# The first 128 columns of the keys' weights as a transfer of their own on ScalarE's queue, in a cross-attention and mixture-of-experts kernel

## The chip, the cores and the metric

The kernel runs on one core of a Trainium2 chip. The metric is the device time of one execution in microseconds (us). A core has five engines that run side by side: TensorE (PE in the profile, its weight loads as PEld), VectorE (DVE), ScalarE (ACT), GpSimd (POOL) and SyncE (SP), which here only issues DMAs. SP, ScalarE and GpSimd can each issue DMAs into a queue of their own; the data is moved by sixteen DMA engines that all queues share. Engines wait for one another, and for DMAs, on semaphores.

## What is computed

Four sequences of 1024 tokens of 256 values attend to a context of 77 rows with 16 heads of 64 values, and the result goes through a mixture of nine experts, of which each token takes two. The part that matters here is the setup of the attention: the context is layer-normed and multiplied with the keys' weights (the first 1024 columns of `Wkv`).

```python
xn = layernorm(x, ln1_w, ln1_b)          # x is the context here, 4 x 77 x 256
ln = layernorm(latents, ln2_w, ln2_b)    # the tokens
q = ln @ Wq
kv = xn @ Wkv
k, v = jnp.split(kv, 2, axis=-1)
...
q = q * (1.0 + scale[:, None, :, None]) + shift[:, None, :, None]
qk = jnp.einsum('bihd,bjhd->bhij', q, k) * attn_scale
attn = jax.nn.softmax(qk, axis=-1)
out = jnp.einsum('bhij,bjhd->bihd', attn, v)
...
x = x + out.reshape(b, -1, INNER) @ Wout
x = x + ffn(layernorm(x), Wr, Wg, Wu, Wd)   # nine experts, the best two of each token
```

All of it is in 32-bit floats.

## The kernel before

The order of the work is written out by hand: each engine executes its instructions in the order in which the program issues them, and only semaphores hold it. There are three stages. The setup, up to about 60 us, folds all weights of the attention into two tables for each sequence, `g` (from context to scores) and `u` (from scores to the output), so that the second stage needs only a few products for each of its 32 blocks of 128 tokens. The third stage runs the experts over lists of tokens that the second stage has written, with the experts' weights streaming in.

The change lies in the first ten microseconds of the setup. What happens there, in order:

- SP issues the loads: the context `cx` in two halves (L381, 77 partitions x 2 x 256 each), the keys' weights `wk_sb` (L382, 128 partitions x 2 x 1024, so 1 MB), the queries' weights `wq_sb` (L383), the values' weights `wv_sb` (L384) and the output's weights `wo_sb` (L385), 1 MB each. L is the line in the kernel.
- ScalarE issues the two small rows `crows` (the context's layer norm, L362) and `frows` (scale and shift, L363), then loads an activation table with a first activation `junk` (L366). Later it issues `wrow` (L473).
- GpSimd issues `qb`, `wr_sb`, `wr_last` and a fill of the token lists in DRAM.
- TensorE runs products on zeros to warm its clock (`warm`, L159), five at once and three more behind `pc` (L418), the turned `crows`.
- VectorE takes the context's statistics (`cst` L404, `cmv` L406), ScalarE the root (`csd` L410), VectorE the reciprocal and most of the normed context `cn` (L456 to L463), ScalarE one quarter of it (L468). TensorE turns it (`pct`, L479), and `cT`, its first half by ScalarE (L488) and its second by VectorE (L483), is what the products need.
- For each of eight pairs of heads, n = 0 to 7, TensorE makes `pk` (L515) of 128 columns of `wk_sb`, from n * 128 on, and `cT`. ScalarE copies the product to `kT` (L519), VectorE scales it into `kTs` (L520). From the fifth pair on, the queries' weights are turned between the pairs (`pwq`, L431), the first reader of `wq_sb`.
- Then come the products for `g` (`pgk`, L651), for `brow` and `u`, up to the first scores at 63 us.

A tile is one block of memory with a name; the tiles `crows`, `frows`, `wrow`, `wq_sb`, `wk_sb` and `cx` come from one pool, `kside`. A read waits for the write of just the part of the tile that it reads. The DMAs of SP and ScalarE share eight semaphores in turn; a DMA that takes a semaphore again waits at its issue until the earlier DMA on it has landed. So `wo_sb` waits at SP for the first half of the context.

The reading side of the weights is this loop:

```python
for n in range(NP):
    pk = bank_tile(f"pk{n}")
    for c in range(C):
        nc.tensor.matmul(
            pk[:, : B * J], wk_sb[:, c, n * P : (n + 1) * P], cT[:, c, :],
            start=(c == 0), stop=(c == C - 1),
        )
```

Of the kernel before, what the change touches and what calls it, by code (L numbers as in the profile page):

```python
# [8 lines left out]
F32 = mybir.dt.float32  # L9
# [6 lines left out]
P = 128  # L16
# [5 lines left out]
def kernel(  # L22
# [18 lines left out]
    nc = tc.nc  # L41
# [4 lines left out]
    INNER = wq.shape[1]  # L46
    DH = INNER // H
    E, _, FF = wg.shape
    C = D // P
# [306 lines left out]
    with tc.tile_pool(name="vside", bufs=1) as vside, ExitStack() as kvs:  # L356
        kside = kvs.enter_context(tc.tile_pool(name="kside", bufs=1))

        crows = kside.tile([2, D], F32, name="crows")
        frows = kside.tile([2, B, NP], F32, name="frows")  # L360
        for k, src in enumerate((ln1_w, ln1_b)):
# [5 lines left out]

        wrow = kside.tile([P, D], F32, name="wrow")
        wq_sb = kside.tile([P, C, INNER], F32, name="wq_sb")
        wk_sb = kside.tile([P, C, INNER], F32, name="wk_sb")  # L370

        QT = 4
        brow = vside.tile([P, NP // QT, B * J], F32, name="brow")
# [5 lines left out]
        for i in range(2):  # L379
            at = slice(i * BH, (i + 1) * BH)  # L380
            nc.sync.dma_start(out=cx[:J, at], in_=ctx_in[at].rearrange("b j d -> j b d"))  # L381
        nc.sync.dma_start(out=wk_sb, in_=wkv[:, :INNER].rearrange("(c p) n -> p c n", p=P))  # L382
        nc.sync.dma_start(out=wq_sb, in_=wq_v)  # L383
        nc.sync.dma_start(out=wv_sb, in_=wkv[:, INNER:].rearrange("(c p) n -> p c n", p=P))  # L384
        nc.sync.dma_start(out=wo_sb[:, :, :D], in_=wout.rearrange("(n p) d -> p n d", p=P))  # L385
# [75 lines left out]
        for b in range(B):  # L461
# [12 lines left out]
            out=wrow, in_=ln2_w.rearrange("(o d) -> o d", o=1).to_broadcast([P, D])  # L474
# [123 lines left out]
        for i in range(2):  # L598
# [4 lines left out]
            out=before, in_=ones, pattern=[[1, P]], compare_op=ALU.is_gt, fill=0.0, base=0,  # L603
# [68 lines left out]
        for b in range(B):  # L672
            nc.vector.tensor_copy(g_sb[b][:, :, HJ:], wz)
            for t in range(2):
                for k in range(NP // QT):
                    nc.sync.dma_start(
                        out=g_sb[b][P - 1 : P, C - 1, :HJ].rearrange(
                            "p (k q t j) -> p k q t j", q=QT, t=2, j=J
                        )[:, k, :, t, :],
                        in_=brow.rearrange("(q r) k m -> q r k m", q=QT)[  # L680
                            :, t * B + b, k, b * J : (b + 1) * J
                        ],
# [871 lines left out]
```

## Time and profile before

| what | us |
|---|---|
| three runs | 924.75, 927.01, 927.33 |
| their median | 927.01 |
| the profiled execution | 924.82 |
| its span, from the first to the last instruction | 922.8 |
| granted TensorE clock, mean, as a share of full speed | 0.997 |

TensorE's time by stage, from the table of stretches:

| stretch | length | TensorE busy |
|---|---|---|
| 0 to 1.5, before the first product | 1.50 | 0.03 |
| 1.5 to 8.8, warming and turning of the context | 7.30 | 7.27 |
| 8.8 to 10.6 | 1.80 | 0.01 |
| 10.6 to 32 | 21.40 | 21.40 |
| 32 to 60 | 28.00 | 28.00 |
| 60 to 480, mostly attention | 420.00 | 415.81 |
| 480 to 900, mostly experts | 420.00 | 419.60 |
| 900 to 922.8 | 22.80 | 14.56 |

In lines of groups and of the timeline, `out<-in` names the tiles, `x` the count and the bracket at the end what the engine waited for, and for how long. A time of a matmul's end is modelled. "SPq" and "ACTq" are DMA issues on SP and ScalarE: the duration is that of issuing, not of the transfer. A row of the table of stretches gives the stretch, its length, then for PE, PEld, DVE, ACT and POOL the busy time and the number of instructions, then the granted TensorE clock, the mean busy share of the DMA engines and the GB/s that they moved.

### The profile page before, as it was taken

How to read it: one execution, taken by the hardware profiler on the slowest of the kernel's cores; microseconds unless marked ns; L12 is line 12 of the kernel's file. 1: busy time of each engine (PE TensorE's matmuls, PEld its weight loads, DVE VectorE, ACT ScalarE, POOL GpSimd, SP SyncE). 2: the span in 40 equal slices, each digit the busy share in tenths (PEclk: the TensorE clock that was granted, in tenths of full speed). 3: DMA queues.
4: the chain of work that ended last, by engine and by line, in shares of the span. 5: the costliest groups of instructions: out<-in, count | busy, mean ns of one | idle time of the engine just before them, and what ended most of it. 6: DMA issues, size and time to landing. Idle time of an engine off the chain costs nothing. (4 is left out here: it accounts for less than half of the span.)

```text
span 922.8 us, 13371 instructions
## 1 busy us (share of the span) xinstructions
PE 906.7 (98%) x4210; PEld 703.5 (76%) x4210; DVE 450.0 (49%) x1330; ACT 341.7 (37%) x1075; POOL 318.2 (34%) x329
## 2 busy tenths in 40 slices
PE   8999999999999999999999999999999999999996
PEld 6676777777777777788888777777777777778885
DVE  5776678888788887763722222222222222222221
ACT  4666575565646566551211122222222222111210
POOL 5000000321504242146454445435435435444432
PEclk9999999999999999999999999999999999999998
DMA  6200010503102710456779779779779777779822
GB/s 216 70 0 1 24 46 25 46 24 46 51 30 59 229 30 24 117 153 172 179 209 299 217 207 307 212 211 313 218 205 310 219 208 227 218 220 312 226 35 23
DMA packets 109125, 137.02 MB, mean 148 GB/s; under 512 B 24247, under 2 KB 79039, under 8 KB 109056
## 3 DMA queue, kind: packets, MB, share of 16 engines
q1 hardware_dynamic: 91498, 118.78, 42.0%
q0 software_dynamic: 17344, 17.26, 10.5%
q8 instruction: 34, 0.56, 0.3%
q14 instruction: 35, 0.29, 0.1%
q10 hardware_dynamic: 214, 0.13, 0.0%
HBM read 119.48 MB, written 18.33 MB: 149 GB/s over the span
## 5 line engine op out<-in xcount | busy, mean ns | idle before, releaser
L1193 PE MATMUL pg<-xT,wgu 128*128 128x256 f32 x1144 | 251.7, 379 | 0.4 <-PEq L1510 0.4
L1193 PEld LDWEIGHTS pg<-xT,wgu 128*128 128x128 f32 x1144 | 215.9, 190 | 29.3 <-issue 0.8
L1267 PE MATMUL po<-wd,hid 128*128 128x256 f32 (+1 forms) x804 | 180.5, 379 | 0.0
L1267 PEld LDWEIGHTS po<-wd,hid 128*128 128x128 f32 (+1 forms) x804 | 147.2, 187 | 21.3 <-issue 0.7
L275 ACT ACTIVATE ex<-psc,mx 128x77 f32<-128x77 f32 x512 | 124.2, 361 | 101.8 <-DVE mx L265 96.7
L1302 POOL DMA_INDIRECT out_dram<-co,ids x63 | 100.7, 1599 | 170.4 <-DVE co L1270 136.4
L918 POOL DMA_INDIRECT list_d<-r_entry,r_pli x64 | 67.2, 1050 | 256.2 <-DVE r_pli L916 124.9
L338 PE MATMUL po<-u,aT 128*128 128x265 f32 x640 | 151.7, 391 | 0.9 <-ACT aT L327 0.8
L261 PE MATMUL psc<-g,zT 128*128 128x462 f32 (+1 forms) x384 | 139.1, 511 | 1.2 <-ACT zT L250 1.2
L338 PEld LDWEIGHTS po<-u,aT 128*128 128x128 f32 x640 | 118.7, 189 | 23.7 <-ACT aT L327 1.9
L1200 DVE TENSOR_TENSOR hid<-pg,sl 128x256 f32<-128x256 f32 x130 | 55.1, 424 | 160.0 <-ACT sl L1199 159.7
L1199 ACT ACTIVATE sl<-pg 128x256 f32<-128x256 f32 x130 | 49.8, 384 | 218.3 <-PE pg L1193 211.9
L261 PEld LDWEIGHTS psc<-g,zT 128*128 128x128 f32 x384 | 72.5, 189 | 59.2 <-issue 49.4
L1270 DVE TENSOR_SCALAR co<-po,ids 128x256 f32<-128x256 f32 x67 | 32.4, 484 | 136.2 <-PE po L1267 136.1
L1151 POOL DMA_INDIRECT yin<-y_d,ids x67 | 70.4, 1051 | 24.7 <-issue 14.7
L265 DVE TENSOR_REDUCE mx<-psc 128x6 f32<-128x462 f32 (+1 forms) x96 | 55.7, 581 | 18.1 <-PE psc L261 15.1
L295 DVE TENSOR_REDUCE sm<-ex 128x16 f32<-128x1232 f32 x32 | 45.9, 1435 | 37.1 <-ACT ex L275 37.1
L327 ACT COPY aT<-pa 128x512 f32<-128x512 f32 (+1 forms) x96 | 49.4, 552 | 26.7 <-PE pa L319 26.7
L319 PEld LDWEIGHTS pa<-ident,an 128*128 128x128 f32 x320 | 36.9, 141 | 7.7 <-PE po L338 1.4
L319 PE MATMUL pa<-ident,an 128*128 128x128 f32 x320 | 40.2, 273 | 1.0 <-DVE an L299 1.0
L299 DVE TENSOR_TENSOR an<-ex,rs 128x1024 f32<-128x1024 f32 x32 | 39.2, 1225 | 1.1
L1255 ACT COPY hid<-ph 128x384 f32<-128x384 f32 x15 | 7.2, 479 | 73.9 <-PE ph L1250 73.9
(312 smaller groups left out, 840.7 us busy)
## 6 DMA issues: line engine op xcount, KB each, us to landing
wgu<-in_L_ffn_Wg_dram SPq DMA_DIRECT2D x41, 704.0 KB
wd<-in_L_ffn_Wd_dram SPq DMA_DIRECT2D x41, 640.0 KB
wgu<-in_L_ffn_Wu_dram SPq DMA_DIRECT2D x41, 512.0 KB
wgu<-in_L_ffn_Wu_dram SPq DMA_DIRECT2D x41, 128.0 KB
x<-in_x_dram SPq DMA_DIRECT2D x8, 512.0 KB
out_dram<-x SPq DMA_DIRECT2D x8, 512.0 KB
y_d<-y SPq DMA_DIRECT2D x8, 512.0 KB
w<-in_L_ffn_Wg_dram SPq DMA_DIRECT2D x5, 704.0 KB
```

The lines of the kernel that those rows point to most:

```text
L261: nc.tensor.matmul(psc[:, :w], zT[:, c, :], g_sb[i // NS // GPB][:, c, h * J : h * J + w], start=(c == 0), stop=(c == C - 1),)
L265: nc.vector.tensor_reduce(nmx[i][:, h : h + n], psc[:, : n * J].rearrange("p (h j) -> p h j", h=n), AX.X, ALU.max, negate=True,)
L275: nc.scalar.activation(exs[i][:, h + q, :], pscs[k][:, q * J : (q + 1) * J], AF.Exp, bias=nmx[i][:, h + q : h + q + 1],)
L319: nc.tensor.transpose(pa[:, q * P : (q + 1) * P], ans[i][:, (k + q) * P : (k + q + 1) * P], ident)
L338: nc.tensor.matmul(po[:, :DE], aT[:, n, :], u_sb[b][:, n, :], start=(n == 0), stop=(n == KC - 1))
L918: i = nc.gpsimd.indirect_dma_start(out=list_d[:, :], out_offset=bass.IndirectOffsetOnAxis(ap=place_i[:, s : s + 1], axis=0), in_=entries[k ...
L1151: return nc.gpsimd.indirect_dma_start(out=dst, out_offset=None, in_=src, in_offset=bass.IndirectOffsetOnAxis(ap=offsets, axis=0), **kw,)
L1193: nc.tensor.matmul(pg[:, g, :], w[:, c, at : at + P], xT[:, c, :], start=(c == 0), stop=(c == C - 1),)
L1199: nc.scalar.activation(sl, pg[:, 0, :], AF.Silu)
L1200: nc.vector.tensor_tensor(hid[:, f, :], pg[:, 1, :], sl, ALU.mult)
L1267: nc.tensor.matmul(po[rows, :D], hid[:, f, at], d[:, f, :], start=(f == 0), stop=(f == NF))
L1302: i = nc.gpsimd.indirect_dma_start(out=out_r, out_offset=bass.IndirectOffsetOnAxis(ap=rows_of(j, h, rows), axis=0), in_=cos[j][:, h, :], i ...
```

## The change

One transfer becomes two. The first 128 columns of the keys' weights, the ones that the first pair reads, are fetched by ScalarE, as its first DMA, before `crows` and `frows`; the other 896 columns are fetched by SP where the whole was before, behind the context. For this the tile `wk_sb` is made at the head of its pool.

```diff
@@ -356,6 +356,10 @@
     with tc.tile_pool(name="vside", bufs=1) as vside, ExitStack() as kvs:
         kside = kvs.enter_context(tc.tile_pool(name="kside", bufs=1))
 
+        wk_sb = kside.tile([P, C, INNER], F32, name="wk_sb")
+        wk_v = wkv[:, :INNER].rearrange("(c p) n -> p c n", p=P)
+
+        nc.scalar.dma_start(out=wk_sb[:, :, :P], in_=wk_v[:, :, :P])
         crows = kside.tile([2, D], F32, name="crows")
         frows = kside.tile([2, B, NP], F32, name="frows")
         for k, src in enumerate((ln1_w, ln1_b)):
@@ -367,7 +371,6 @@
 
         wrow = kside.tile([P, D], F32, name="wrow")
         wq_sb = kside.tile([P, C, INNER], F32, name="wq_sb")
-        wk_sb = kside.tile([P, C, INNER], F32, name="wk_sb")
 
         QT = 4
         brow = vside.tile([P, NP // QT, B * J], F32, name="brow")
@@ -379,7 +382,7 @@
         for i in range(2):
             at = slice(i * BH, (i + 1) * BH)
             nc.sync.dma_start(out=cx[:J, at], in_=ctx_in[at].rearrange("b j d -> j b d"))
-        nc.sync.dma_start(out=wk_sb, in_=wkv[:, :INNER].rearrange("(c p) n -> p c n", p=P))
+        nc.sync.dma_start(out=wk_sb[:, :, P:], in_=wk_v[:, :, P:])
         nc.sync.dma_start(out=wq_sb, in_=wq_v)
         nc.sync.dma_start(out=wv_sb, in_=wkv[:, INNER:].rearrange("(c p) n -> p c n", p=P))
         nc.sync.dma_start(out=wo_sb[:, :, :D], in_=wout.rearrange("(n p) d -> p n d", p=P))
```

## The prediction

> **What bounds the kernel now.** I read the page first (part 1, then the slices of part 2), then the list of waits for the first 70 us, the timeline of the first 13 us, and the table of stretches for those. The page:
>
> ```profile
> span 922.8 us, 13371 instructions
> PE 906.7 (98%) x4210; PEld 703.5 (76%) x4210; DVE 450.0 (49%) x1330; ACT 341.7 (37%) x1075; POOL 318.2 (34%) x329
> ```
>
> TensorE is counted busy for all but 922.8 - 906.7 = 16.1 us. Nothing that removes waits from it can give more, and a change in the setup can only give what TensorE idles there. The waits:
>
> ```profile
> PE pk L515 <- DMA wk_sb<-in_L_xattn_Wkv_dram: 1.8, 1, 1.8
> PE warm L159 <- DVE u L155: 1.5, 1, 1.5
> ```
>
> The setup has two idle stretches on TensorE: 1.5 us of start, and 1.8 us in front of the first product with the keys' weights. Only the second concerns this change. In the table of stretches TensorE is busy for 49.00 of the 49.00 us from 11 to 60, so a shift at 11 us is passed on. How the 1.8 us come about is in the timeline (start, duration, engine, line, operation):
>
> ```profile
> 0.83 0.81 SPq L381 DMA_DIRECT2D cx<-in_ctx_dram  x2
> 0.84 0.52 ACTq L362 DMA_DIRECT2D crows<-in_L_xattn_ln_w_dram  x1
> 1.69 0.44 SPq L382 DMA_DIRECT2D wk_sb<-in_L_xattn_Wkv_dram  x1
> 3.91 1.40 DVE L404 BATCH_NORM_STATS2 cst<-cx 77x6 f32<-77x256 f32 x4 [2.23 <-DMA cx<-in_ctx_dram]
> 6.24 1.05 DVE L463 TENSOR_SCALAR cn<-cx,cmv,cr 77x256 f32<-77x256 f32 x3
> 6.33 1.56 PE L159 MATMUL warm<-u 128*128 128x256 f32 x6
> 7.73 0.70 PE L479 MATMUL pct<-ident,cn 77*128 77x77 f32 x8
> 8.20 0.61 ACT L488 ACTIVATE cT<-pct,cwb 128x308 f32<-128x308 f32 x1 [1.25 <-PE pct L479]
> 8.47 0.60 DVE L483 TENSOR_SCALAR cT<-pct,cwb 128x308 f32<-128x308 f32 x1 [1.11 <-PE pct L479]
> 10.60 2.57 PE L515 MATMUL pk<-cT,wk_sb 128*128 128x308 f32 x9 [1.83 <-DMA wk_sb<-in_L_xattn_Wkv_dram]
> ```
>
> Two inputs meet at 10.60: the turned context cT, ready at 8.20 + 0.61 = 8.81 (first half) and 8.47 + 0.60 = 9.07 (second), and wk_sb, which comes last. The trace's semaphore records put the sixteen parts of the wk_sb landing between 7.71 and 10.46. What the DMA engines did meanwhile (last columns: granted clock, DMA share, GB/s):
>
> ```profile
> 2.50:2.75 0.25, 0.25 (x2) 0.25 (x1) 0.00 (x0) 0.25 (x1) 0.25 (x1) 1.00 0.72 254
> 3.75:4.00 0.25, 0.25 (x2) 0.23 (x1) 0.09 (x1) 0.00 (x0) 0.25 (x1) 1.00 0.04 4
> 4.00:4.50 0.50, 0.50 (x2) 0.41 (x2) 0.50 (x2) 0.00 (x0) 0.50 (x2) 1.00 0.69 41
> 4.50:5.00 0.50, 0.50 (x2) 0.36 (x2) 0.50 (x3) 0.00 (x0) 0.21 (x1) 1.00 0.57 57
> 6.00:6.50 0.50, 0.50 (x4) 0.45 (x4) 0.47 (x3) 0.14 (x1) 0.00 (x0) 1.00 0.91 360
> 9.00:10.00 1.00, 0.00 (x0) 0.00 (x0) 0.54 (x4) 0.00 (x0) 0.87 (x1) 1.00 1.01 392
> ```
>
> The reader should see three things: the context moves at about 254 GB/s, then between 3.75 and 5 us almost nothing moves although wk_sb was issued at 1.69, and then the queue runs at 360 to 392. In the packet records the first wk_sb packet on most engines took 1.1 to 2.3 us and later ones about 0.16; that is the gap.
>
> [...] No printed view shows which engine a packet ran on; but queue 10 (ScalarE's) and queue 1 (SP's) packets do overlap around 3 us. [...] 11 late increments for a context half, 16 for wk_sb, five of these at 7.71 to 7.84, ahead of the rest.
>
> **The change part by part.**
>
> Added: one DMA of 128 x 2 x 128 floats = 131 KB on ScalarE's queue, in front of crows and frows. Issuing the like costs 0.44 us on SP, so crows, frows and the table load move back by some 0.45 us. Their covers: crows had landed at 4.08 and TensorE reads them at 6.03; frows at 5.55, read at 8.36; the table load and its activation end at 3.43 and ScalarE's next work begins at 5.62. Even with 0.6 us more behind the slice in the ring they hold. Cost 0; if crows passed 6.0, the six warming products and all behind them would slip with them.
>
> Cut: wk_sb on SP's queue falls to 128 x 2 x 896 floats = 918 KB, in runs of 3584 bytes. The compiled program's waits are as the words say: the first pair's product waits for the slice's semaphore, the second pair's for the rest. One more follows from the reuse of semaphores: wv_sb, issued at 2.68 before without a wait, now waits on SP for the slice, and wo_sb behind it for one of the crows instead of the context. Both are read from 32.9 us on and had landed by 16.7 and 19.6: cost 0.
>
> Context beside the slice. Not in the trace, so from both sides. Least: 0, as the engines run at 35 to 127 GB/s from 1.5 to 2.5. A gain is excluded: nothing ahead of the context goes away. Most: the slice's first packets hold their engines as those of wk_sb did, about 2 us. I take the sharing of bytes alone: 131 KB at 390 GB/s = 0.34 us. Behind it the chain statistics, root, cn is dense, but TensorE ends the warming products only at about 7.5 (first weight load of pct at 7.52) while cn is done at 7.29, so 0.2 is covered: 0.14 remains.
>
> First pair: from cT at 8.81 + 0.05 to issue + 0.14 = 9.0, if the slice is there. It was asked for at 0.84; even 2 us of first packet and 1 us of data leave it at 5. The pair takes 1.04 us (kT copies stand 1.04 apart), so the second pair could start at 10.04.
>
> Rest: wk_sb ran on the slow engines from about 5.0 to 10.46; an eighth less is 0.69 less, and the slice adds 0.34 in front if it does not fit into the gap: 10.46 - 0.69 + 0.34 = 10.1, and 0.14 to TensorE's start as before = 10.25. Bounds: 9.3, if the slice has already paid for the first packets; 10.6[...]. The second pair started at 10.60 + 1.04 = 11.64; at 10.25 it gains 1.4.
>
> What is late next: wq_sb. Its last part landed at 14.14 and TensorE loads it first at 15.60; 1.4 earlier is 14.20, just at the landing plus 0.14. Its bytes ahead are the same, so I cap the gain at 1.3. The next, wrow, landed at 13.50 for a use at 16.90. GpSimd's clearing of vbd starts with cT's second half and ends 17 us ahead of its use.
>
> Sum: 924.82 for the profiled execution (922.8 of span and 2.0 around it) - 1.3 = 923.5. The three runs have a median of 927.01, which is 2.2 above that execution; against them 927.0 - 1.3 = 925.7.
>
> **The rivals.**
>
> The rest becomes the wait: slice and rest together carry the same bytes, the total is bound by the engines at 390 GB/s[...], so the rest lands at 10.4 to 11.0. For it: a share of 1.0 from 8 us on. Against: the empty stretch at 3.75 to 5. Second pair at about 11.1, gain 0.5: 926.5.
>
> The context pays: it lands 0.9 late instead of 0.34, 0.7 beyond the cover, first pair at 9.6, second at 10.6 or later: gain 1.0 at most and 0.7 if the rest slips by the same 0.3. [...] Time 926.3.
>
> The other side: the slice's first packets stall the engines under the context for their full 2 us. Then cT comes 1.8 late, at 10.6, the first pair starts at 10.7 and 10.9 if the second half is the late one, and all behind is 0.1 to 0.3 slower: 927.2. It decides from a context delay of 10.60 - 8.86 + 0.2 = 1.9 us on. Against it: frows' 4-byte packets went through at 3.5 to 5.2, while wk_sb's first packets hung.
>
> That the change does not act at all would need the first product to wait for both parts; the program's waits exclude it.
>
> **How the numbers follow.** Forecast 0.55; rest as the wait 0.2; context pays 0.15; the slower one 0.1. All lie within 1.5 us of the median, and 0.3% (2.8 us) is about what a measurement of this kernel can tell from no change. The three runs before span 2.6 us, so a median moves by a microsecond of its own accord. Gains of 1.3 with that scatter, and an unknown settling of later transfers against each other, pass 2.8 in about 2 of 10; a loss of 2.8 needs the slower case plus scatter: 0.06. The range takes 0.3 of loss and 1.7 of gain (TensorE's whole wait) with 1 to 2 us of scatter: 923.2 to 927.9.
>
> **What would show it.** Wait of pk for wk_sb at its first product gone or below 0.3; a second wait on the rest of at most 0.3 at the second pair; bn_stats on the context at 4.1 to 4.4; kT's first copy at about 10.2 instead of 11.91, the second at 11.5 instead of 12.94; pwq's first load near 14.3. The forecast is wrong if the statistics start after 5.5, or if the second pair waits beyond 11.2, or if the products before 16 us come 1.3 earlier and the end does not.

## The result, and the profile after

The changed kernel takes 930.88 us (median of six runs, 930.29 to 934.63), the kernel before 925.07 us beside it; the ratio is 1.0062, with a 95% interval of 1.0042 to 1.0082. The change costs 5.8 us. The profiled execution of the changed kernel took 930.29 us. Its page (span; busy time and share of the span by engine):

```profile
span 928.3 us, 13375 instructions
PE 908.7 (98%) x4210; PEld 704.6 (76%) x4210; DVE 449.8 (48%) x1330; ACT 340.8 (37%) x1075; POOL 320.1 (34%) x329
```

TensorE is busy for 2.0 us more than before with the same 4210 products, and the span is 5.5 us longer, so it also idles 3.5 us more. The list of TensorE's waits for the first 70 us names the place:

```profile
PE pfs L500 <- DMA frows<-in_fside_Bx_dram: 5.5, 1, 5.5
PE warm L159 <- DVE u L155: 1.5, 1, 1.5
```

The wait of the first product for the keys' weights is gone, as the change meant it. In its place stands one for `frows`, the 64 values of scale and shift, which did not show at all before. The timeline of the first 18 us (start, duration, engine, line, operation, and in the bracket what it waited for):

```profile
0.84 0.43 ACTq L362 DMA_DIRECT2D wk_sb<-in_L_xattn_Wkv_dram  x1
2.15 0.30 ACTq L367 DMA_DIRECT2D frows<-in_fside_Bx_dram  x1
...
4.28 0.75 DVE L407 BATCH_NORM_STATS2 cst<-cx 77x6 f32<-77x256 f32 x2 [2.60 <-DMA cx<-in_ctx_dram]
5.68 0.75 DVE L407 BATCH_NORM_STATS2 cst<-cx 77x6 f32<-77x256 f32 x2 [0.65 <-DMA cx<-in_ctx_dram]
8.13 0.89 PE L482 MATMUL pct<-ident,cn 77*128 77x77 f32 x8 [0.68 <-ACT cn L471]
9.06 0.60 DVE L486 TENSOR_SCALAR cT<-pct,cwb 128x308 f32<-128x308 f32 x1 [0.58 <-PE pct L482]
14.52 0.60 PE L500 MATMUL pfs<-frows,two 2*128 2x32 f32 x2 [5.50 <-DMA frows<-in_fside_Bx_dram]
15.04 3.45 PE L518 MATMUL pk<-cT,wk_sb 128*128 128x308 f32 x6
```

The context is turned and ready at 9.06 + 0.60 = 9.66. The slice had landed at 4.69 and the rest of the weights at 8.88 (semaphore records), so all that `pk` reads is there. But `pfs`, a product of 0.6 us, stands in front of `pk` in TensorE's order and waits for `frows`, issued at 2.15 and landed at 14.38. The first pair starts at 15.04 instead of 10.60: 4.44 us late.

The table of stretches shows the rest of the loss and a part of its cause. After the span and length come PE, PEld, DVE, ACT, POOL, and at the end the granted TensorE clock, the DMA engines' busy share and GB/s:

```profile
3.75:4.00 0.25, 0.25 (x2) 0.23 (x1) 0.00 (x0) 0.22 (x2) 0.25 (x1) 1.00 0.80 279
4.00:4.50 0.50, 0.50 (x2) 0.41 (x2) 0.22 (x1) 0.00 (x0) 0.50 (x2) 1.00 1.18 346
12.00:14.50 2.50, 0.00 (x0) 0.01 (x1) 0.00 (x0) 0.00 (x0) 2.50 (x3) 0.50 0.96 352
15.00:18.00 3.00, 3.00 (x7) 2.08 (x7) 0.61 (x4) 0.41 (x1) 3.00 (x27) 0.50 0.86 293
```

First, the gap of before is closed: 279 and 346 GB/s from 3.75 to 4.5, where 4 and 41 GB/s stood. Why it is closed is not shown; the last section comes back to it. Secondly, TensorE's clock is halved; the clock records say from 12.01 to 18.83. In the three microseconds from 15 on it makes seven products. The last copy to `kT` ends the eight pairs. In the kernel before, and in the changed one:

```profile
20.48 0.42 ACT L519 COPY kT<-pk 128x308 f32<-128x308 f32 x1 [0.26 <-PE pk L515]
```

```profile
26.82 0.41 ACT L522 COPY kT<-pk 128x308 f32<-128x308 f32 x1 [0.26 <-PE pk L518]
```

It starts 6.34 us late. So 4.44 us are the later start and 6.34 - 4.44 = 1.90 us the halved clock; this is half of the 18.83 - 15.04 = 3.79 us that the products run at half clock. At the first copy of `brow` the delay is still 6.33 (38.83 against 32.50); at the end 5.5 are left. TensorE idles 0.9 us less between 60 and 480 us than before; which waits of the later stages took the delay up was not traced further.

### The profile page after: what moved, and what is told of

Read it like the earlier page. It is cut to its first block, busy times and chain, and to the rows that moved or that the text cites. A ratio compares the mean times of both kernels' runs of the same rounds, so it can differ in the third digit from the quotient of the medians.

```text
span 928.3 us, 13375 instructions
## 1 busy us (share of the span) xinstructions
PE 908.7 (98%) x4210; PEld 704.6 (76%) x4210; DVE 449.8 (48%) x1330; ACT 340.8 (37%) x1075; POOL 320.1 (34%) x329
## 4 chain that ended last, share of the span: by engine, by line
PE 86%; DMA 5%; issue 3%; DVE 2%; POOL 1%; ACT 1%; SPq 0%; POOLq 0%; ACTq 0%
PE pg L1196 21%; PE po L1270 16%; PE po L338 15%; PE psc L261 14%; PE pa L319 3%; PE psg L1232 3%; PE psu L1232 3%; PE psb L1232 2%; DMA out_dram<-co,ids 2%; PE px L1182 2%; PE pu L742 1%; DMA frows<-in_fside_Bx_dram 1%; PE pk L518 1%; PE ph L1253 1%; DMA wd_r<-in_L_ffn_Wd_dram 1%
```

## The experiments

My theory after the trace: `frows` is 64 packets of 4 bytes (the packet records show them on ScalarE's queue). Before, they went through at 3.50 to 5.22, in the gap. Now all go through from 6.48 to 13.93, while the DMA engines have a busy share of 0.96 and move 339 GB/s, most of it the bulk of another queue; that is 7.45 us for 64 packets, 0.12 us from one to the next on average, while a bulk packet takes 0.17 to 0.18 on average and one of 4 bytes 0.009. The rivals were the delayed context, a fixed cost of the slice, and small packets being slow anywhere.

The experiments ran on four chips. On three of them the kernel before took 924.3 to 924.9 us (medians); on the fourth, that of the first four experiments, 929.94 with a spread from 926.8 to 933.7. Ratios from that chip are weak, and I rest only on traces of it.

**rows_first**: the slice behind the three small rows.

```diff
-        nc.scalar.dma_start(out=wk_sb[:, :, :P], in_=wk_v[:, :, :P])
         crows = kside.tile([2, D], F32, name="crows")
...
         nc.scalar.dma_start(out=frows, in_=fside.rearrange("b (n t) -> t b n", t=2))
+        nc.scalar.dma_start(out=wk_sb[:, :, :P], in_=wk_v[:, :, :P])
```

> The change with ScalarE's three small rows issued ahead of the slice instead of behind it; nothing else differs. Theory (frows' 64 packets of 4 bytes are stuck behind the bulk of the weights): frows lands by about 6 us as before, the 5.5 us wait of pfs goes, TensorE stays at full clock, and the time is 923.5 to 925.0, at least 5.5 us under the changed kernel. Rival (the slice delays the context, and that is what costs): the context is as late as in the changed kernel, and the time stays at 929 to 931.

Measured 930.45 us, ratio 0.9999 (0.9984 to 1.0015): no difference that this chip's scatter lets one see. Its list of TensorE's waits:

```profile
PE pk L518 <- DMA wk_sb<-in_L_xattn_Wkv_dram: 2.8, 1, 2.8
PE pfs L500 <- DMA frows<-in_fside_Bx_dram: 1.5, 1, 1.5
```

The wait for `frows` falls from 5.5 to 1.5, and now the slice is what is late: its 256 packets ran from 4.27 to 12.10, those of the changed kernel from 2.15 to 3.91. In this trace, what ScalarE's queue still held while SP's bulk ran was stretched, at 512 bytes as at 4. My expectation of 923.5 to 925.0 was wrong. The time lies in the rival's range, but not for the rival's reason: the turned context was ready at 9.08, as in the kernel before (9.07). And `frows`, ahead of the slice and issued at 1.63 as before, still landed only at 9.81.

**before_frows_late**, twice: the kernel before, with `frows` behind ScalarE's first activation in the program.

```diff
-        nc.scalar.dma_start(out=frows, in_=fside.rearrange("b (n t) -> t b n", t=2))
         junk = const.tile([P, 1], F32, name="junk")
         nc.scalar.activation(junk, eps_t, AF.Sqrt)
+        nc.scalar.dma_start(out=frows, in_=fside.rearrange("b (n t) -> t b n", t=2))
```

> The kernel before, keys' weights in one transfer, with frows issued behind ScalarE's first activation, at about 3.2 us instead of 1.64. No slice. Theory (frows only has to miss the gap before the bulk of the weights starts): frows lands at 11 to 15 us, pfs waits 3 to 6 us, and the time is 928 to 931. Rival (it is the slice ahead of frows in ScalarE's queue that holds it): frows lands by 7.5 us and the time stays at 925.1 within 0.7.

> The kernel of before_frows_late once more on the chip of this call: frows alone is issued some 1.5 us later, no slice. Its profile showed a wait of 4.0 us of pfs for frows. Theory: a ratio of 1.003 to 1.006. Rival: within 0.999 to 1.001.

Measured 931.18 us, ratio 1.0012 (0.9995 to 1.0028), and on a calmer chip 925.74, ratio 1.0004 (0.9995 to 1.0013). The waits of the first one's trace, and of the second one's:

```profile
PE pfs L497 <- DMA frows<-in_fside_Bx_dram: 4.0, 1, 4.0
```

```profile
PE pk L515 <- DMA wk_sb<-in_L_xattn_Wkv_dram: 2.5, 1, 2.5
```

The edit did not do what I meant by it. The issue did not wait for the activation: the traces show it at 1.70 and 1.69, where the kernel before has 1.64. From the second trace:

```profile
1.69 0.26 ACTq L366 DMA_DIRECT2D frows<-in_fside_Bx_dram  x1
...
2.92 0.20 ACT L365 ACTIVATE junk<-eps_t 128x1 f32<-128x1 f32 x1
```

So these are, in effect, two more executions of the kernel before. In one, on the chip with the wide spread, `frows` was caught by the bulk without any slice and landed at 11.71; in the other its packets passed from 3.45 to 3.77, and it landed at 4.39. Whether a late issue alone would do harm was not put to the test. The expected 1.003 to 1.006 was wrong, and the rival's 0.999 to 1.001 held.

**after_warm** and **after_warm15**: the changed kernel with ten and with fifteen more products on zeros in front of `pfs`.

```diff
+        warm(range(WARM, WARM + 15))
         pfs = bank_tile("pfs")
```

> The changed kernel with ten more warming products on zeros in front of pfs (about 5.2 us of work at full clock), the wait for frows left as it is. Theory (part of the loss is TensorE's clock, halved after its idle wait): the clock stays at full speed after 12 us, pfs is where it was, about 14.5, and the 1.9 us that the eight products lose at half clock come back: 928.7 to 929.3. Rival (the time is lost in the wait alone, or the warming products push pfs back): 930.5 to 931.5.

> The changed kernel with fifteen warming products in front of pfs, enough to fill its whole wait for frows (ten took 4.2 us and left 2.3 us idle). Theory (about 1.8 of the 5.8 us are TensorE's halved clock behind the wait): full clock up to the end, the products pk at 1.04 us each from the first, and a ratio to the kernel before of 1.003 to 1.0045. Rival (the clock is not a part of it): 1.0055 to 1.0065.

Measured 930.92, ratio 1.0007 (0.9991 to 1.0023) with ten, where 2.3 us of the wait stayed and the clock still fell, from 15.92 to 19.33; and 930.41, ratio 1.0064 (1.0051 to 1.0077), with fifteen. Stretches of the changed kernel, profiled once more as **after_again**, and then of after_warm15:

```profile
8.00:14.50 6.50, 0.00 (x0) 0.00 (x0) 0.57 (x1) 0.31 (x1) 5.87 (x4) 0.79 1.01 386
15.00:18.00 3.00, 3.00 (x8) 2.05 (x8) 0.56 (x3) 0.36 (x1) 2.00 (x25) 0.50 0.75 246
```

```profile
8.00:14.50 6.50, 6.50 (x35) 5.78 (x34) 0.60 (x1) 0.61 (x1) 5.42 (x4) 1.00 1.01 379
15.00:18.00 3.00, 3.00 (x13) 2.27 (x14) 1.05 (x5) 0.83 (x2) 2.46 (x26) 1.00 0.81 273
```

With the wait filled, the clock stays at 1.00 and the same three microseconds hold thirteen products instead of eight; the span is 926.0 instead of 927.8. That the idle wait halves the clock is shown, and in the trace it gives back 1.7 us: the last copy to `kT` starts at 25.08, in after_again at 26.79. Its price in the median is not shown: five runs of after_warm15 spread from 928.3 to 931.5, the profiled one being the quickest, and their ratio is no better than the changed kernel's. By the times, the rival held in both runs. All five have a mean granted clock of 0.996 to 0.998, the six of after_again 0.992 to 0.994, so it is not the clock that made the other four slower; what did stays open.

> The changed kernel itself once more, beside the kernel before on the chip of the experiments, where the kernel before runs at 926.8 to 933.7 us. Theory ([...]): the changed kernel is at 930 to 934, a ratio of 1.000 to 1.006. Rival (the loss is a fixed 5.8 us): 935.0 to 936.5, a ratio of 1.0062.

after_again measured 930.2 us, ratio 1.0058 (1.0043 to 1.0073), with a wait of 6.7 us for `frows`. The loss repeats in a second set of runs, although the turned context was ready at 8.57 there, 0.5 us earlier than in the first profile of the kernel before and 0.9 earlier than in before_again on the same chip (9.46): the rival of the delayed context falls with that. The kernel was not tried on the chip with the wide spread, so that expectation was not put to the test there.

**before_again**: the kernel before, unchanged.

> The kernel before, profiled where it is slow. Theory: its profile shows the same wait that the changed kernel shows, pfs for frows or the first product for the weights at 11.5 to 15 us, and half a clock behind it. Rival (the chip is slower all along): no such wait, and the time is spread over the attention and the experts.

Measured 924.5 us, ratio 0.9995 (0.9987 to 1.0003), on a chip where it is not slow: it cannot say why the other chip was. The runs' clocks give a hint: of the 44 runs of the kernel before on that other chip, the eleven slowest have a mean granted clock of 0.993 to 0.996, the eleven fastest 0.997 or 0.998. A wait like that in the first trace of before_frows_late would fit, but no slow run of the unchanged kernel was profiled.

**split_on_sp**: both parts on SP's queue, behind the context, ScalarE's queue as before.

```diff
-        nc.sync.dma_start(out=wk_sb, in_=wkv[:, :INNER].rearrange("(c p) n -> p c n", p=P))
+        nc.sync.dma_start(out=wk_sb[:, :, :P], in_=wk_v[:, :, :P])
+        nc.sync.dma_start(out=wk_sb[:, :, P:], in_=wk_v[:, :, P:])
```

> Both parts of the keys' weights on SP's queue behind the context, the 128 columns first; ScalarE's queue as in the kernel before, frows in 64 packets. Theory: frows stays as exposed as before, so the time is that of the kernel before less up to 1 us of the first pair's earlier start: ratio 0.998 to 1.001. Rival (what matters is only when the slice lands): 1.5 us and more under the kernel before, a ratio below 0.998.

Measured 923.66 us, ratio 0.9983 (0.9974 to 0.9992). Its timeline:

```profile
9.40 1.27 PE L518 MATMUL pk<-cT,wk_sb 128*128 128x308 f32 x4 [0.18 <-ACT cT L491]
...
11.71 4.38 PE L518 MATMUL pk<-cT,wk_sb 128*128 128x308 f32 x16 [1.04 <-DMA wk_sb<-in_L_xattn_Wkv_dram]
```

The split by itself does no harm: `frows` landed at 4.63. The first pair starts 1.2 us earlier, and the second waits 1.04 us for the rest. That is the prediction's first rival, in which the rest becomes the wait. By the medians the gain of 1.3 us is just beyond the 1 us that I expected, by the ratio it is within; no gain is left at the second pair of this one execution (11.71 against 10.62 + 1.04 in before_again), so where it comes from is not shown.

**rows_on_sp**: the slice stays first on ScalarE's queue; the three small rows go to SP's, between the context and the rest.

```diff
-            nc.scalar.dma_start(out=crows[k : k + 1, :], in_=src.rearrange("(o d) -> o d", o=1))
-        nc.scalar.dma_start(out=frows, in_=fside.rearrange("b (n t) -> t b n", t=2))
...
+            nc.sync.dma_start(out=crows[k : k + 1, :], in_=src.rearrange("(o d) -> o d", o=1))
+        nc.sync.dma_start(out=frows, in_=fside.rearrange("b (n t) -> t b n", t=2))
         nc.sync.dma_start(out=wk_sb[:, :, P:], in_=wk_v[:, :, P:])
```

> The changed kernel with the three small rows taken off ScalarE's queue and issued on SP's, between the context and the rest of the keys' weights; frows is still 64 packets of 4 bytes, the slice is still first on ScalarE. Theory (it is not the size of the packets alone but that they stand in another queue than the bulk[...]): in one queue, ahead of the bulk, they pass at once; frows lands by 6 us, no wait of pfs, first pair at 9 to 9.8, ratio to the kernel before 0.997 to 1.000. Rival (4-byte packets are slow in any queue): frows after 9.5 us and a ratio above 1.002.

Measured 923.63 us, ratio 0.9989 (0.9980 to 0.9997). Its timeline:

```profile
8.83 0.40 PE L500 MATMUL pfs<-frows,two 2*128 2x32 f32 x2
...
9.33 5.45 PE L518 MATMUL pk<-cT,wk_sb 128*128 128x308 f32 x20
```

The same 64 packets landed at 5.96, `pfs` does not wait, and the first five pairs follow without a break, though this edit also moved the issue of the rest from 1.69 to 2.61. So it is not the size of the packets alone: in the bulk's own queue and ahead of it they pass.

**after_frows_row**, twice: the changed kernel with `frows` as one row of 256 bytes, still behind the slice on ScalarE's queue.

```diff
-        frows = kside.tile([2, B, NP], F32, name="frows")
+        frows = kside.tile([1, B * H], F32, name="frows")
-        nc.scalar.dma_start(out=frows, in_=fside.rearrange("b (n t) -> t b n", t=2))
+        nc.scalar.dma_start(out=frows, in_=fside.rearrange("(o b) h -> o (b h)", o=1))
...
-        nc.tensor.matmul(
-            pfs[:, : B * NP], two.rearrange("r t p -> r (t p)"),
-            frows.rearrange("r b n -> r (b n)"), start=True, stop=True,
-        )
+        for t in range(2):
+            nc.tensor.matmul(
+                pfs[:, : B * NP], two[:, t, :], frows.rearrange("o (m t) -> o t m", t=2)[:, t, :],
+                start=(t == 0), stop=(t == 1),
+            )
```

> The changed kernel with frows loaded as one row of 64 values, 256 bytes on one partition, and spread to 128 partitions by two products with a row of ones and zeros each instead of one; it is still issued behind the slice. Theory (64 packets of 4 bytes[...] are the cost): one packet lands by about 6 us, the wait goes, 923.5 to 925.0. Rival (anything on ScalarE's queue behind the slice lands late, whatever its packets): frows lands after 9.5 us still and the time is above 927.

> The kernel of after_frows_row once more, since its chip ran the kernel before at 929.9 with a wide scatter. Theory: frows as one packet removes the wait whatever the chip; on a chip where the kernel before is at 925 it is at 924 to 926.5, a ratio of 0.999 to 1.0015 (crows, two packets, still lands late behind the slice and delays pc by about 1 us). Rival (a fixed cost of the slice remains): 928 and more, a ratio above 1.003.

Measured 925.09 us, ratio 0.9952 (0.9931 to 0.9974), where the kernel before spread widely, and 922.52, ratio 0.9971 (0.9964 to 0.9979), on a calm chip. The second one's timeline:

```profile
8.03 0.63 PE L503 MATMUL pfs<-frows,two 1*128 1x32 f32 x4
...
8.59 5.45 PE L521 MATMUL pk<-cT,wk_sb 128*128 128x308 f32 x20
```

One packet lands at 6.74 where 64 landed at 14.38, in the same place of the same queue. With that the changed kernel is faster than both kernels of this case, by 0.0029 * 924.76 = 2.7 us against the kernel before (2.2 by the medians): the first pair starts at 8.59, 2.0 us earlier than at 10.60, and the rest had landed at 8.63, before the second. That is better than the 0.999 to 1.0015 that I expected: `crows` landed at 4.64 there, and `pc` did not wait for it.

**before_frows_row**: the same edit of `frows` in the kernel before.

> The kernel before, keys' weights in one transfer, with frows as one row of 256 bytes, as in after_frows_row. Theory: the 64 packets of 4 bytes were what scattered the kernel before too; 924 to 926.5, at least 3 us under it and as fast as after_frows_row within 1.5. Rival (it is the early slice that made after_frows_row fast): as the kernel before, within 1 us.

Measured 926.09 us, ratio 1.0010 (0.9998 to 1.0021), with a wait of 1.8 us for the keys' weights as ever. There the row gains nothing; it is a cure for the slice's side effect. The rival held by the ratio (0.9 us); by the medians it is 1.2.

**frows_ahead**: in the changed kernel, `frows` alone moved to the head of ScalarE's queue, then the slice, then `crows`.

```diff
+        nc.scalar.dma_start(out=frows, in_=fside.rearrange("b (n t) -> t b n", t=2))
         nc.scalar.dma_start(out=wk_sb[:, :, :P], in_=wk_v[:, :, :P])
...
-        nc.scalar.dma_start(out=frows, in_=fside.rearrange("b (n t) -> t b n", t=2))
```

> The changed kernel with frows alone moved, from the end of ScalarE's small rows to the head of its queue, in front of the slice; still 64 packets of 4 bytes. Theory (its place behind the slice is what made it late): frows lands by 4 us, pfs does not wait for it, the first pair starts by 9.7 us, and the ratio to the kernel before is 0.996 to 1.000, unless the slice, issued 0.5 us later, is late in its turn. Rival (4-byte packets on ScalarE's queue are held up by the bulk wherever they stand): frows after 9.5 us and a ratio above 1.004.

Measured 924.86 us, ratio 0.9999 (0.9985 to 1.0013). Its list of TensorE's waits:

```profile
PE pc L421 <- DMA crows<-in_L_xattn_ln_b_dram: 1.1, 1, 1.1
```

No wait for `frows`, which landed at 4.24, and the loss of 5.8 us is gone. `crows`, last in the queue, landed at 7.09, and `pc` in front of the warming products pays for it. The three warming products behind `pc` then took 2.93 us instead of 1.56, as the clock came to full speed only at 11.09 (in the kernel before at 6.27). So the first pair starts at 11.64, not by 9.7. The edit moves both the place of `frows` and its issue, from 2.15 to 0.83: in front of the slice and issued that early, it is not late.

**rows_on_sp_row**: rows_on_sp, with `frows` as one row as well.

> rows_on_sp with frows as one packet as well. Theory (both cures remove the same wait): no wait of pfs for frows, the ratio to the kernel before 0.996 to 0.999, not below that of after_frows_row_b (0.9971) by more than 0.001. Rival (two separate costs): below 0.9955.

Measured 923.15 us, ratio 0.9983 (0.9975 to 0.9990). The cures don't add up: they remove the same wait.

## Why the prediction was wrong

A gain of 1.3 us was forecast, and a loss of 5.8 was measured. The step that failed is the cover of the small rows in "Added": "frows at 5.55, read at 8.36 [...] Even with 0.6 us more behind the slice in the ring they hold. Cost 0". By this, `frows` would have landed at 5.55 + 0.45 + 0.6 = 6.6 at the latest; it landed at 14.38. The step took the lateness of a row on the queue for the slice's own bytes and some issue time. What it should have counted was packets: the trace before shows 64 packets of 4 bytes, and that they had passed while the engines moved little, 58 GB/s on average from 3.50 to 5.22. At 339 GB/s in the changed kernel they came one by one, some 0.1 us apart (at 8.79, 8.91, 8.99, 9.07, 9.16), and took 7.45 us. Why they came no faster is not shown: no view names the engine of a packet, or the order in which an engine serves the queues. So the forecast's first packets that hold their engines are my reading of the packet times as well. That in these runs the number of packets and the queue decide is shown by after_frows_row_b, where one packet landed at 6.74, and rows_on_sp, where 64 on SP's queue landed at 5.96.

The slice is not the only way into this wait. With the slice ahead of the 64 packets on ScalarE's queue, `frows` landed at 14.38 to 14.69 in all four traces (after, after_again, after_warm, after_warm15). Without it ahead on that queue, it landed at 4.39 to 5.76 in before, before_again, before_frows_late_b and split_on_sp, but at 9.81 and 11.71 in rows_first and before_frows_late, on the chip with the wide spread. So a place behind the slice was enough in every trace that has it, but it is not needed; what delays `frows` on that chip without it stays open.

The text even had the gap in hand. It counted the gap's closing as a possible gain for the rest of the weights, and did not ask who else lived in it. And it used frows' passing "at 3.5 to 5.2" as evidence against a stall, without seeing that these were the packets that passed in the gap.

The second part, a halved clock after the wait, 1.90 us in the profile, was not foreseen at all, because the wait was not.

The other steps:

- Slice, first pair: right. It landed at 4.69, and the wait of `pk` for weights is gone.
- Context beside the slice: 0.34 late was forecast; the statistics started 0.37 late (4.28 against 3.91). But the second half came later, with a wait of 0.65 of its own, and `cT` was 0.59 late instead of 0.14. In after_again it was not late at all (8.57 against 9.07 of the first profile), so the size is a matter of the execution.
- Rest: forecast at 10.1, bounds 9.3 and 10.6; landed at 8.88, below the bound. The term that was mis-sized is the first packets': thirteen packets of before took 1.1 to 2.3 us, and of the rest's none took more than 0.51. The slice did not take that time over: its packets took 0.03 to 0.18 us each.
- `crows`: forecast to hold up to 6.0 us. It landed at 5.57 in the changed kernel and held; in frows_ahead it was 7.09 and did not.
- The gain of 1.3 that the sum came to is there once `frows` is out of the way: by the medians 1.1 us in rows_on_sp and 2.2 in after_frows_row_b.
- The slower rival was given the wrong place: the context. The place was a transfer of 256 bytes in the same queue, and its price 5.5 us of wait instead of 0.3.

## What to carry to other kernels

A transfer that is moved to the head of a queue can delay what stands behind it, and for the small transfer of this case the delay went by packets, not bytes (the same 256 bytes landed at 14.38 in 64 packets and at 6.74 in one): look up how many packets it has and what else runs while they pass. Ask of every gap in the DMA engines that a change closes, which transfers used to pass in it. Where many tiny packets are needed early, make them one, or put them in front of the bulk in the bulk's own queue; in rows_on_sp the 64 then landed at 5.96.

## What the runs showed of the hardware that was not expected

A load of 64 single floats, 256 bytes in all, took 12.2 us from issue to landing while the DMA engines moved 339 GB/s, most of it bulk from another queue (6.48 to 13.93); as one packet in the same place it took 4.6 us (after_frows_row_b, issued at 2.15, landed at 6.74).

In the kernel before, thirteen packets of the keys' weights took 1.1 to 2.3 us each, and most others 0.16. With an eighth of them fetched apart and 0.85 us earlier, the rest landed at 8.88 instead of 10.46. The cause is open. It is not that the first reads of a tensor are slow as such: the first sixteen packets of `wq_sb`, which nothing had read before, took 0.16 to 0.17 us each in the changed kernel, and in before_frows_row, without a slice, no packet of `wk_sb` took more than 0.90 us. Nor does an early slice close the gap by itself: in rows_on_sp the engines moved 72 and 79 GB/s from 4.0 to 5.0, though the slice had gone through by 3.4.

TensorE's granted clock fell to half with the wait of 5.5 us in the changed kernel: its last product before the wait ended at 9.02, and the clock was 0.50 from 12.01 to 18.83. With the 1.8 us of the kernel before it stayed at 1.00. With the 2.5 us of before_frows_late_b it fell: the first copies to `kT` behind the wait start 1.88 us apart, the later ones 1.03 to 1.04 (12.26, 14.14, 16.02, 17.05, 18.09). The half clock lasted 6.83 us in the changed kernel and 3.41 us in after_warm (15.92 to 19.33). How much idle time it takes to bring the clock down, and what sets the length of the stretch, is not shown by these few waits.
